# Layer-1 experts of a two-layer graph transformer: results added to rows of the output by accumulating scatters

## The chip, the cores and the metric

The kernel runs on one core of a Trainium2 chip. The metric is device time in microseconds (us), the median of several runs. The names used below: PE is TensorE (matrix products), DVE is VectorE, ACT is ScalarE, POOL is GpSimd and SP is SyncE, which here only issues loads. All engines read and write on-chip memory in tiles of 128 partitions (rows); matrix products land in PSUM banks. Transfers to and from DRAM are DMAs, issued by SP, ACT or POOL and carried out by 16 shared DMA engines. Every engine works through its own instructions in order. An instruction waits until the semaphores of what it needs have come.

## The reference

Two layers work on 384 nodes with 1024 features. Each layer adds a graph attention and a mixing block to x, and then a mixture of experts. All numbers are 32-bit floats. The change touches the experts of the second layer (layer 1), which the reference computes thus:

```python
aff = feats @ centroids.T
eid = jnp.argmax(aff, axis=1)
...
xhat = (feats - mu) * jax.lax.rsqrt(var + EPS)
out = jnp.zeros_like(feats)
for e in range(E):
    mask = (eid == e).astype(feats.dtype)[:, None]
    h = xhat * gamma[e] + beta[e]
    y = feats + jax.nn.relu(h @ w1[e] + b1[e]) @ w2[e] + b2[e]
    alpha = jax.nn.sigmoid(feats @ centroids[e])[:, None]
    out = out + mask * (alpha * y + (1.0 - alpha) * feats)
```

Here feats is the layer norm of x. Each node has exactly one of E = 8 experts, and the final output is x + out. For a node of expert e that comes to

x + feats + alpha * (relu(h @ w1[e] + b1[e]) @ w2[e] + b2[e]).

So there is a base, x + feats, which no expert touches, and a product scaled by alpha. The expert's bias b2[e] is scaled by alpha too.

## The kernel before, in words

**Blocks and places.** The 384 nodes lie in three blocks (nb) of 128 rows. The experts are worked sorted: every expert has CAP = 64 places, and a node's place (slot) is 64 * expert + its rank among the nodes of that expert. Two experts make a pair of 128 places, and four pairs follow each other. Places without a node keep a blank row index, so that what is written through them is dropped.

**Routing, at the end of `layer1`.** For a block, `project` multiplies by w_fc (L1117). `mix_norm` finishes x (L1128, L1129). `to_router` transposes x (`to_t`, L217 and L218), multiplies it by the centroids (L1151), and writes ft (feats) and xb (the normed feats). `to_places` finds the expert (one-hot oh, by `first_of`), the rank (`place`, a product with `later` or `ones_q`, L328), the slot and own (L1181, a one-hot over the 128 places of pair 0). It scatters xb by slot to the DRAM table xg. POOL then adds x + ft (L1184), and that base row is scattered by slot to the DRAM table bg. `to_first` multiplies xb by own (L1189), which gives pair 0's rows already transposed, in PSUM. In the code `to_router` of the last block comes first, then `to_first` of blocks 0 and 1, then `to_places` and `to_first` of the last. `scaled` (L974 and L975 on DVE, L981 on ACT) applies gamma and beta to pair 0's rows and writes xe0. Last, info, that is alpha and the node's row number, is scattered to ig.

**Experts, `experts1_sorted`.** POOL loads the four pairs' base rows back from bg (base) and loads ig (inf); ACT loads b2. For each pair the code runs:

- w1 of both experts is loaded by SP (`load_w`, 2 MB each).
- For pairs 1 to 3, xs is loaded by SP from xg and transposed (L1321), and `scaled` gives xeT. Pair 0 takes xe0.
- h = xeT * w1: 16 products (L1326). Each takes 64 places, and each appears in the profile as two passes, as 32-bit products do.
- ACT copies h to hs (L1329). It is transposed (L1335), and bias b1 and relu give hT (DVE L1343, ACT L1341).
- y = hT * w2 in two halves of 512 features, 8 products each (L1350). One more product per half adds b2 through `pick`, which names the expert of each place (L1352).
- o = y * alpha + base (L1354). One scatter by row number writes o to out (L292).

Each row of out is written once, by the pair that holds its node.

**The weight places.** `next_w` takes the 2 MB places for weights in turn from `ring`. Three stand in the ring from the start, and w_top, w_more (two) and w_last were added on the way, so that seven rotate here. A load can start when the last product that reads the place's former weights is done.

**Order.** A scheduler places the instructions of each engine. It may move work of one engine past other work, as the transposes L1321 of the next pair show, which stand ahead of y. `issue_after` sets an order by hand.

Of the kernel before, what the change touches and what calls it, by code (L numbers as in the profile page):

```python
# [10 lines left out]
F32 = mybir.dt.float32  # L11
I32 = mybir.dt.int32
AF = mybir.ActivationFunctionType
OP = mybir.AluOpType
# [30 lines left out]
def gps_two_layers(ctx: ExitStack, tc: tile.TileContext, d, out: bass.AP):  # L45
# [45 lines left out]
    bg = dram.tile([X * CAP, D], F32, name="bg")  # L91
    ig = dram.tile([X * CAP, 2], F32, name="ig")
    x1 = dram.tile([N, D], F32, name="x1")

# [151 lines left out]
    def first_of(onehot, vals, most):  # L246

        eq = small.tile([P, X], F32, tag="fo_e", name="fo_e")
        ve.scalar_tensor_tensor(eq, vals, most, ridx, op0=OP.is_equal, op1=OP.mult)
        c = small.tile([P, 1], F32, tag="fo_c", name="fo_c")  # L250
        ve.tensor_reduce(c, eq, AX.X, OP.max)
        ve.tensor_scalar(onehot, ridx, c, None, op0=OP.is_equal)

    def gate_to_t(pool, tag, gate):
        gT = small.tile([X, N], F32, tag="gT", name="gT", bufs=1)
# [29 lines left out]

    sent = {}

    def scatter(rows, ats, srcs, n):

        before = sent.setdefault(rows.tensor.name, [])  # L290
        for at, src in zip(ats, srcs):
            i = gp.indirect_dma_start(rows, bass.IndirectOffsetOnAxis(ap=at, axis=0), src, None,  # L292
                                      bounds_check=n - 1, oob_is_err=False)
            for j in before:
                tc.declare_no_dep(i.ins, j.ins, reason="no two nodes have one place")
            before.append(i)
        return i
# [15 lines left out]

    def blanks(q, blank):

        for t, n in ((xg0, X * CAP0), (xg, X * CAP), (bg, X * CAP)):
            for i in range(n // P):
                q.dma_start(t[i * P:(i + 1) * P, :], blank[:, :D])
        blank_i = const.tile([P, 2], I32, name="blank_i")
        gp.memset(blank_i, 1 << 20)  # L320
        for i in range(X * CAP // P):
            q.dma_start(ig[i * P:(i + 1) * P, :], blank_i.bitcast(F32))
# [91 lines left out]
    with ExitStack() as layer:  # L414
# [317 lines left out]
        def row(cols, name, dtype=F32):  # L732
            return kp.tile([P, *cols], dtype, name=name)

        keep = {"xe0": [row([KC // 2, P], f"xe0_{g}") for g in range(2)], "oh": row([NB, X], "oh4"), "own": row([NB, P], "own4"), "most": row([NB], "most4"),
                "slot": row([NB], "slot4", I32), "info": row([NB, 2], "info4"),
                "slots": row([NB, 2], "slots6", I32), "share": row([2, NB], "share6")}


# [243 lines left out]
    def layer1(keep=None):  # L983


        with tc.tile_pool(name="act2", bufs=1) as act, \
# [303 lines left out]

    def experts1_sorted(xe0):

        with tc.tile_pool(name="act4", bufs=1) as act, \
# [5 lines left out]
            b2 = act.tile([X, D], F32, name="b24")  # L1299
            ac.dma_start(b2, d["b2"])  # L1300
            pick = act.tile([X, X * CAP], F32, name="pick4")
            gp.tensor_copy(pick.rearrange("p (a b) -> p a b", b=CAP), ident[:X, :X][:, :, None].to_broadcast([X, X, CAP]))
            base = act.tile([P, X // 2, D], F32, name="base4")
            for pair in range(X // 2):
                gp.dma_start(base[:, pair, :], bg[pair * P:(pair + 1) * P, :])
                if pair == 0:
                    gp.dma_start(inf, ig.rearrange("(a p) b -> p a b", p=P))
            for pair in range(X // 2):
                es = (2 * pair, 2 * pair + 1)
                rows = slice(pair * P, (pair + 1) * P)  # L1310
                w1 = [load_w(d["xw1"][e]) for e in es]
                xeT = xe0
                if pair:
                    xs = work.tile([P, D], F32, tag="xs", name="xs4")
                    nc.sync.dma_start(xs, xg[rows, :])
                    xeT = [work.tile([P, KC // 2, P], F32, tag=f"xeT{g}", name="xeT4") for g in range(2)]
                    for g in range(2):
                        ps = pt.tile([P, HB], F32, tag="t", name="t4").rearrange("p (a b) -> p a b", b=P)
                        for j in range(4):
                            kc = g * 4 + j  # L1320
                            nc.tensor.transpose(ps[:, j, :], xs[:, kc * P:(kc + 1) * P], ident)  # L1321
                        scaled(xeT[g], ps, g, es)
                h = ph.tile([P, HB], F32, tag="h", name="h4")
                for kc in range(KC):
                    for r in range(2):
                        mm(h[r * CAP:(r + 1) * CAP, :], lhsT=xeT[kc // 4][:, kc % 4, r * CAP:(r + 1) * CAP], rhs=w1[r][:, kc, :],  # L1326
                           start=kc == 0, stop=kc == KC - 1)
                hs = work.tile([P, F1], F32, tag="hs", name="hs4")
                ac.copy(hs, h)  # L1329
                w2 = [load_w(d["xw2s"][e], (F1 // P, D)) for e in es]  # L1330
                hT = work.tile([P, F1 // P, P], F32, tag="hT", name="hT4")
                for g in range(2):
                    ps = pt.tile([P, HB], F32, tag="t", name="t4").rearrange("p (a b) -> p a b", b=P)
                    for j in range(2):
                        nc.tensor.transpose(ps[:, j, :], hs[:, (2 * g + j) * P:(2 * g + j + 1) * P], ident)  # L1335
                    for j in range(2):
                        for r, e in enumerate(es):
# [6 lines left out]
                y = [py.tile([P, HB], F32, tag="y", name="y4") for _ in range(2)]  # L1344
                o = work.tile([P, D], F32, tag="o", name="o4")
                for hf in range(2):
                    cs = slice(hf * HB, (hf + 1) * HB)
                    for j in range(F1 // P):
                        for r in range(2):
                            mm(y[hf][r * CAP:(r + 1) * CAP, :], lhsT=hT[:, j, r * CAP:(r + 1) * CAP],  # L1350
                               rhs=w2[r][:, j, cs], start=j == 0, stop=False)
                    mm(y[hf], lhsT=pick[:, pair * P:(pair + 1) * P],  # L1352
                       rhs=b2[:, cs], start=False, stop=True)
# [114 lines left out]
```

## Time and profile before

| what | us |
|---|---|
| median of 3 runs | 1074.85 |
| lowest and highest of them | 1074.51, 1077.58 |
| the profiled execution | 1074.58 |
| its span, first to last instruction | 1072.9 |
| PE busy | 1021.7 (95% of the span) |
| DVE, ACT, POOL busy | 346.0, 270.8, 317.8 |
| first expert product of layer 1 starts | 982.90 |
| first expert product of pairs 1, 2, 3 | 1004.99, 1026.79, 1047.17 |
| last product ends | 1065.38 |
| last scatter of out issued | 1066.45 |

The profile is of one execution. Its span leaves out 1.7 us of the time that was measured for that execution. Line numbers are those of the kernel before. "x32" counts instructions as the hardware ran them; a product of 32-bit floats counts as two. "Landing" is the time from the issue of a transfer to its completion. The granted clock is the share of full speed at which PE ran: 1.00 for most of the span, and 0.50 from 964 to 972 us.

### The profile page before, as it was taken

How to read it: one execution, taken by the hardware profiler on the slowest of the kernel's cores; microseconds unless marked ns; L12 is line 12 of the kernel's file. 1: busy time of each engine (PE TensorE's matmuls, PEld its weight loads, DVE VectorE, ACT ScalarE, POOL GpSimd, SP SyncE). 2: the span in 40 equal slices, each digit the busy share in tenths (PEclk: the TensorE clock that was granted, in tenths of full speed). 3: DMA queues.
4: the chain of work that ended last, by engine and by line, in shares of the span. 5: the costliest groups of instructions: out<-in, count | busy, mean ns of one | idle time of the engine just before them, and what ended most of it. 6: DMA issues, size and time to landing. Idle time of an engine off the chain costs nothing.

```text
span 1072.9 us, 9493 instructions
## 1 busy us (share of the span) xinstructions
PE 1021.7 (95%) x3453; PEld 554.1 (52%) x3453; DVE 346.0 (32%) x960; ACT 270.8 (25%) x499; POOL 317.8 (30%) x276
## 2 busy tenths in 40 slices
PE   6999999999999999999989999959999999988996
PEld 5555555544555555544466665424444466545332
DVE  4580000007676666701251110142205002463121
ACT  3111111100966666611131111221311111112111
POOL 2142365556685778500001000230002000024000
PEclk9999999999999999999999999979999999997999
DMA  9939623235326232541357888975540224244991
GB/s 346 402 126 391 199 79 134 102 103 102 75 1 158 33 47 1 158 162 44 128 206 261 312 303 309 361 260 205 195 141 17 78 83 153 79 170 148 392 411 59
DMA packets 69973, 186.01 MB, mean 173 GB/s; under 512 B 21416, under 2 KB 22280, under 8 KB 69664
## 3 DMA queue, kind: packets, MB, share of 16 engines
q1 hardware_dynamic: 41648, 149.68, 38.7%
q0 software_dynamic: 24688, 29.40, 11.1%
q10 hardware_dynamic: 3584, 6.25, 1.5%
q8 instruction: 29, 0.48, 0.2%
q14 instruction: 24, 0.20, 0.1%
HBM read 160.77 MB, written 25.06 MB: 173 GB/s over the span
## 4 chain that ended last, share of the span: by engine, by line
PE 92%; DVE 4%; DMA 1%; ACT 1%; issue 1%; POOL 0%; POOLq 0%; ACTq 0%; DVEq 0%
PE mm L136 23%; PE mm L148 12%; PE mm L666 11%; PE mm L714 8%; PE h L916 7%; PE mm L1012 4%; PE mm L1117 4%; PE y L943 4%; PE h L1326 3%; PE y L1350 3%; PE av L653 2%; PE sc L624 2%; PE tr L647 2%; PE x L1057 1%; PE mm L217 1%
## 5 line engine op out<-in xcount | busy, mean ns | idle before, releaser
L480 POOL DMA_INDIRECT countd<-seen,cells x96 | 153.9, 1603 | 64.4 <-DMA countd<-seen,cells 39.4
L136 PE MATMUL mm<-xnT,w 128*128 128x384 f32 x512 | 165.7, 486 | 0.0
L666 PE MATMUL mm<-xnT,w 128*128 128x384 f32 x384 | 132.4, 493 | 0.0
L136 PEld LDWEIGHTS mm<-xnT,w 128*128 128x128 f32 x512 | 97.1, 190 | 67.5
L480 POOL DMA_INDIRECT lastd<-typ,cells x96 | 95.7, 997 | 113.0 <-DMA lastd<-typ,cells 75.8
L666 PEld LDWEIGHTS mm<-xnT,w 128*128 128x128 f32 x384 | 70.5, 190 | 56.4 <-issue 13.4
L714 PE MATMUL mm<-w,t 128*128 128x512 f32 x192 | 84.3, 595 | 0.8 <-DVE x L402 0.8
L148 PE MATMUL mm<-w,xnT 128*128 128x512 f32 x192 | 82.8, 592 | 0.0
L136 PE MATMUL mm<-t,w 128*128 128x384 f32 x256 | 82.7, 486 | 0.0
L916 PE MATMUL h<-w,xeT 128*128 128x352 f32 x224 | 68.3, 462 | 0.7 <-DVE xeT L908 0.3
L136 PEld LDWEIGHTS mm<-t,w 128*128 128x128 f32 x256 | 48.6, 190 | 33.9
L148 PEld LDWEIGHTS mm<-w,xnT 128*128 128x128 f32 x192 | 36.3, 190 | 45.5 <-issue 45.5
L714 PEld LDWEIGHTS mm<-w,t 128*128 128x128 f32 x192 | 35.9, 190 | 44.1 <-issue 42.2
L586 DVE TENSOR_TENSOR kind<-last 128x1152 f32<-128x1152 f32 x1 | 1.4, 1358 | 167.7 <-DMA last<-lastd 167.7
L916 PEld LDWEIGHTS h<-w,xeT 128*128 128x128 f32 x224 | 41.9, 190 | 24.4 <-DVE xeT L908 2.4
L292 POOL DMA_INDIRECT xg<-xn,slot x3 | 4.0, 1324 | 144.0 <-DVE xn L1128 122.6
L1012 PE MATMUL mm<-w,xnT 128*128 128x512 f32 x96 | 43.7, 615 | 1.3 <-DVE xnT L218 1.3
L1117 PE MATMUL mm<-w,oT 128*128 128x512 f32 x96 | 42.6, 595 | 0.0
L943 PE MATMUL y<-w,hT 128*128 128x512 f32 (+1 forms) x96 | 41.6, 592 | 0.0
L148 PE MATMUL mm<-w,t 128*128 128x512 f32 x96 | 41.4, 592 | 0.0
L527 ACT ACTIVATE t<-mm,cols 128x384 f32<-128x384 f32 x24 | 13.9, 581 | 106.7 <-PE mm L136 106.7
L1067 POOL TENSOR_TENSOR x<-x,gb 128x1024 f32<-128x1024 f32 x3 | 7.3, 2423 | 99.2 <-DVE x L1066 99.2
(296 smaller groups left out, 1194.2 us busy)
## 6 DMA issues: line engine op xcount, KB each, us to landing
w<-in_w1s SPq DMA_DIRECT2D x16, 1408.0 KB, 7.1
w<-in_xw SPq DMA_DIRECT2D x8, 2048.0 KB, 12.3
w<-in_xw2s SPq DMA_DIRECT2D x8, 2048.0 KB, 13.7
w<-in_w2s SPq DMA_DIRECT2D x8, 1536.0 KB, 7.1
keys<-keyd POOLq DMA_DIRECT2D x4, 1536.0 KB, 14.3
xg<-blank SPq DMA_DIRECT2D x12, 512.0 KB, 11.0
w<-in_wk SPq DMA_DIRECT2D x2, 2048.0 KB, 15.8
w<-in_mwq SPq DMA_DIRECT2D x2, 2048.0 KB, 11.1
```

The costliest lines, as they stand in the source:

```text
L136: mm(ps[:, :N], lhsT=w[:, j, kc, :], rhs=rhs[:, kc, :], start=kc == 0, stop=kc == KC - 1)
L148: mm(ps, lhsT=lhs[:, kc, nb * P:(nb + 1) * P], rhs=w[:, kc, :], start=i == 0 and kc == 0, stop=i == len(pairs) - 1 and kc == KC - 1)
L480: gp.indirect_dma_start(cells[:, :], bass.IndirectOffsetOnAxis(ap=at[:, i, c:c + 1], axis=0), src[:, c:c + 1], None, bounds_check=N * N + ...
L624: mm(ps[:, r, :N], lhsT=q2T[rows, hp, nb * P:(nb + 1) * P], rhs=k2T[rows, hp, :], start=True, stop=True)
L666: mm(ps[:, :N], lhsT=w[:, j, kc, :], rhs=xnT[:, kc, :], start=kc == 0, stop=kc == KC - 1)
L714: mm(pss[hf], lhsT=src[:, kc, nb * P:(nb + 1) * P], rhs=w_out[("mwo", "wo")[part]][hf][:, kc, :], start=part == 0 and kc == 0, stop=part = ...
L916: mm(ag[i][:, :F0], lhsT=xeT[kc // 4][:, kc % 4, :], rhs=w1[kc // 4][:, kc % 4, i * F0:(i + 1) * F0], start=kc == 0, stop=kc == KC - 1)
L943: mm(y, lhsT=hT[:k, e, j, :], rhs=w2[:k, e % 2 * len(K2) + j, :], start=j == 0, stop=j == len(K2) - 1)
L1012: mm(ps, lhsT=xnT[:, kc, nb * P:(nb + 1) * P], rhs=ws[hf][:, kc, :], start=kc == 0, stop=kc == KC - 1)
L1117: mm(ps, lhsT=oT[:, kc, nb * P:(nb + 1) * P], rhs=ws[hf][:, kc, :], start=kc == 0, stop=kc == KC - 1)
L1326: mm(h[r * CAP:(r + 1) * CAP, :], lhsT=xeT[kc // 4][:, kc % 4, r * CAP:(r + 1) * CAP], rhs=w1[r][:, kc, :], start=kc == 0, stop=kc == KC - 1)
L1350: mm(y[hf][r * CAP:(r + 1) * CAP, :], lhsT=hT[:, j, r * CAP:(r + 1) * CAP], rhs=w2[r][:, j, cs], start=j == 0, stop=False)
```

## The change

The base rows are no longer sorted. The table bg is gone, with its blanks, its three scatters and its four loads. The base x + ft stays in on-chip memory in the order of the nodes: POOL makes it for blocks 0 and 1, DVE for the last block. Every node's own bias row is gathered from b2 by the expert's number (own_e), multiplied by alpha and added, and ACT stores the result to out. The experts then only *add* to out: y * alpha goes out by scatters with compute_op add, two per pair, one for each half of 512 features (half holds 2 * row + half). They wait for the three base stores. The product with `pick` is gone.

`to_first` of block 0 now stands before the last `to_router`, and that of block 1 right behind it. The rows of all pairs are loaded early, by POOL and no longer by SP. The next pair's rows are transposed inside the y of pair 0, and between h and hs of pairs 1 and 2. The copy hs is divided between DVE and ACT. The ring gets one more place, w_end.

```diff
 def first_of(onehot, vals, most):
...
+        return c
...
-    def scatter(rows, ats, srcs, n):
+    def scatter(rows, ats, srcs, n, op=OP.bypass):
...
-                                      bounds_check=n - 1, oob_is_err=False)
+                                      bounds_check=n - 1, oob_is_err=False, compute_op=op)
...
-        for t, n in ((xg0, X * CAP0), (xg, X * CAP), (bg, X * CAP)):
+        for t, n in ((xg0, X * CAP0), (xg, X * CAP)):
...
-                first_of(oh[:, nb, :], near, top)
+                c = first_of(oh[:, nb, :], near, top)
...
-                with tc.issue_after(scatter(xg[:, :], [slot[:, nb:nb + 1]], [xb], X * CAP).ins):
-                    gp.tensor_tensor(x[:, nb, :], x[:, nb, :], fb, OP.add)
-                    last[:] = [scatter(bg[:, :], [slot[:, nb:nb + 1]], [x[:, nb, :]], X * CAP)]
+                ve.tensor_scalar(keep["own_e"][:, nb:nb + 1], c, -1.0, float(X), op0=OP.mult, op1=OP.add)
+                last[:] = [scatter(xg[:, :], [slot[:, nb:nb + 1]], [xb], X * CAP)]
+                if nb < NB - 1:
+                    with tc.issue_after(last[0].ins):
+                        gp.tensor_tensor(x[:, nb, :], x[:, nb, :], fb, OP.add)
...
+            to_first(0)
             to_router(NB - 1)
-            for nb in range(NB - 1):
-                to_first(nb)
+            to_first(1)
             to_places(NB - 1)
             to_first(NB - 1)
...
+            ve.tensor_tensor(x[:, NB - 1, :], x[:, NB - 1, :], ft[:, NB - 1, :D], OP.add)
...
+            ring.append(w_end)
...
+            def load_rows(pair):
+                xs = work.tile([P, D], F32, tag="xs", name="xs4", bufs=3)
+                gp.dma_start(xs, xg[pair * P:(pair + 1) * P, :])
+                return xs
...
+            def hidden_of(pair, xeT):
...
-                ac.copy(hs, h)
+                ve.tensor_copy(hs[:, :F1 // 2], h[:, :F1 // 2])
+                ac.copy(hs[:, F1 // 2:], h[:, F1 // 2:])
...
+            def give(pair, hT, between=None):
...
-                    mm(y[hf], lhsT=pick[:, pair * P:(pair + 1) * P],
-                       rhs=b2[:, cs], start=False, stop=True)
-                    ve.scalar_tensor_tensor(o[:, cs], y[hf], inf[:, pair, 0:1], base[:, pair, cs],
-                                            op0=OP.mult, op1=OP.add)
-                scatter(out[:, :], [inf[:, pair, 1:2].bitcast(I32)], [o], N)
+                    o = work.tile([P, HB], F32, tag="o", name="o4", bufs=4)
+                    ve.tensor_scalar(o, y, inf[:, pair, 0:1], None, op0=OP.mult)
+                    scatter(out.rearrange("n (h f) -> (n h) f", h=2), [half[:, hf, pair:pair + 1]], [o], 2 * N, OP.add)
+                    if hf == 0 and between is not None:
+                        got = rows_of(between)
...
+            xss = [None] + [load_rows(pair) for pair in range(1, X // 2)]
+            gp.dma_start(inf, ig.rearrange("(a p) b -> p a b", p=P))
+            for nb in range(NB):
+                gather(b2[:, nb, :], d["b2"], keep["own_e"][:, nb:nb + 1], X)
+            hs = hidden_of(0, xe0)
+            for hf in range(2):
+                ve.tensor_scalar(half[:, hf, :], inf[:, :, 1].bitcast(I32), 2.0, float(hf), op0=OP.mult, op1=OP.add)
+            for nb in range(NB):
+                ve.scalar_tensor_tensor(x[:, nb, :], b2[:, nb, :], keep["info"][:, nb, 0:1], x[:, nb, :],
+                                        op0=OP.mult, op1=OP.add)
+                ac.dma_start(out[nb * P:(nb + 1) * P, :], x[:, nb, :])
+            xeT = give(0, by_feature(0, hs), 1)
+            for pair in range(1, X // 2):
+                hs = hidden_of(pair, xeT)
+                if pair + 1 < X // 2:
+                    xeT = rows_of(pair + 1)
+                give(pair, by_feature(pair, hs))
```

In the built program the new instructions stand thus on their engines: on DVE the two `half` steps ahead of pair 0's hs, the first addition of a bias row between the second and third hT piece of pair 0, the other two around the first scaling step of pair 1's rows; on ACT the base stores behind pair 0's hT, among the scaling steps of pair 1's rows; on POOL, after the last scatters to xg and ig, the loads xs, inf, the three gathers and the scatters of out.

More of the change, by code (lines that the diff above doesn't have):

```diff
@@ L90, in gps_two_layers @@
     xg = dram.tile([X * CAP, D], F32, name="xg")
-    bg = dram.tile([X * CAP, D], F32, name="bg")
     ig = dram.tile([X * CAP, 2], F32, name="ig")
@@ L735, in gps_two_layers @@
         keep = {"xe0": [row([KC // 2, P], f"xe0_{g}") for g in range(2)], "oh": row([NB, X], "oh4"), "own": row([NB, P], "own4"), "most": row([NB], "most4"),
-                "slot": row([NB], "slot4", I32), "info": row([NB, 2], "info4"),
+                "slot": row([NB], "slot4", I32), "own_e": row([NB], "own_e4", I32), "info": row([NB, 2], "info4"),
                 "slots": row([NB, 2], "slots6", I32), "share": row([2, NB], "share6")}
@@ L1291, in experts1_sorted @@
     def experts1_sorted(xe0):
-        with tc.tile_pool(name="act4", bufs=1) as act, \
+        with tc.tile_pool(name="w_end", bufs=1) as w_end, \
+                tc.tile_pool(name="act4", bufs=1) as act, \
                 tc.tile_pool(name="work5", bufs=2) as work, \
@@ L1297, in experts1_sorted @@
                 tc.tile_pool(name="ps_y4", bufs=2, space=PSUM) as py:
+            ring.append(w_end)
             inf = act.tile([P, X // 2, 2], F32, name="inf4")
[L1299 to L1322, printed above, removed]
+            half = act.tile([P, 2, X // 2], I32, name="half4")
@@ new lines, in experts1_sorted, with rows_of @@
+            b2 = act.tile([P, NB, D], F32, name="b24")
+            def load_rows(pair):
+                xs = work.tile([P, D], F32, tag="xs", name="xs4", bufs=3)
+                gp.dma_start(xs, xg[pair * P:(pair + 1) * P, :])
+                return xs
+            def rows_of(pair):
+                xeT = [work.tile([P, KC // 2, P], F32, tag=f"xeT{g}", name="xeT4") for g in range(2)]
+                for g in range(2):
+                    ps = pt.tile([P, HB], F32, tag="t", name="t4").rearrange("p (a b) -> p a b", b=P)
+                    for j in range(4):
+                        kc = g * 4 + j
+                        nc.tensor.transpose(ps[:, j, :], xss[pair][:, kc * P:(kc + 1) * P], ident)
+                    scaled(xeT[g], ps, g, (2 * pair, 2 * pair + 1))
+                return xeT
@@ L1323, in experts1_sorted @@
+            def hidden_of(pair, xeT):
+                w1 = [load_w(d["xw1"][e]) for e in (2 * pair, 2 * pair + 1)]
                 h = ph.tile([P, HB], F32, tag="h", name="h4")
@@ L1328, in experts1_sorted, with by_feature @@
                 hs = work.tile([P, F1], F32, tag="hs", name="hs4")
-                ac.copy(hs, h)
-                w2 = [load_w(d["xw2s"][e], (F1 // P, D)) for e in es]
+                ve.tensor_copy(hs[:, :F1 // 2], h[:, :F1 // 2])
+                ac.copy(hs[:, F1 // 2:], h[:, F1 // 2:])
+                return hs
+            def by_feature(pair, hs):
                 hT = work.tile([P, F1 // P, P], F32, tag="hT", name="hT4")
@@ L1336, in experts1_sorted @@
                     for j in range(2):
-                        for r, e in enumerate(es):
+                        for r, e in enumerate((2 * pair, 2 * pair + 1)):
                             f, cs = 2 * g + j, slice(r * CAP, (r + 1) * CAP)
@@ L1343, in experts1_sorted @@
                                 ve.tensor_scalar(hT[:, f, cs], ps[:, j, cs], bias, 0.0, op0=OP.add, op1=OP.max)
-                y = [py.tile([P, HB], F32, tag="y", name="y4") for _ in range(2)]
-                o = work.tile([P, D], F32, tag="o", name="o4")
+                return hT
+            def give(pair, hT, between=None):
+                w2 = [load_w(d["xw2s"][e], (F1 // P, D)) for e in (2 * pair, 2 * pair + 1)]
                 for hf in range(2):
                     cs = slice(hf * HB, (hf + 1) * HB)
+                    y = py.tile([P, HB], F32, tag="y", name="y4")
@@ L1348, in experts1_sorted @@
                     for j in range(F1 // P):
                         for r in range(2):
-                            mm(y[hf][r * CAP:(r + 1) * CAP, :], lhsT=hT[:, j, r * CAP:(r + 1) * CAP],
-                               rhs=w2[r][:, j, cs], start=j == 0, stop=False)
-                    mm(y[hf], lhsT=pick[:, pair * P:(pair + 1) * P],
-                       rhs=b2[:, cs], start=False, stop=True)
-                    ve.scalar_tensor_tensor(o[:, cs], y[hf], inf[:, pair, 0:1], base[:, pair, cs],
-                                            op0=OP.mult, op1=OP.add)
@@ L1356, in experts1_sorted @@
-                scatter(out[:, :], [inf[:, pair, 1:2].bitcast(I32)], [o], N)
+                            mm(y[r * CAP:(r + 1) * CAP, :], lhsT=hT[:, j, r * CAP:(r + 1) * CAP],
+                               rhs=w2[r][:, j, cs], start=j == 0, stop=j == F1 // P - 1)
+                    o = work.tile([P, HB], F32, tag="o", name="o4", bufs=4)
+                    ve.tensor_scalar(o, y, inf[:, pair, 0:1], None, op0=OP.mult)
+                    scatter(out.rearrange("n (h f) -> (n h) f", h=2), [half[:, hf, pair:pair + 1]], [o], 2 * N, OP.add)
@@ new lines, in give @@
+                    if hf == 0 and between is not None:
+                        got = rows_of(between)
+                return got if between is not None else None
+            xss = [None] + [load_rows(pair) for pair in range(1, X // 2)]
[5 more added lines that the diff above has]
+                ve.tensor_scalar(half[:, hf, :], inf[:, :, 1].bitcast(I32), 2.0, float(hf), op0=OP.mult, op1=OP.add)
```

## The prediction

> **What bounds the kernel now.** I read the page's chain first, then the chain in order of time from 960 us, the waits of PE, and last the stretches with the DMA share.
>
> ```profile
> PE 92%; DVE 4%; DMA 1%; ACT 1%; issue 1%; POOL 0%; POOLq 0%; ACTq 0%; DVEq 0%
> ```
>
> PE holds 92% of the chain, so time is saved where PE loses work or a wait, and nowhere else. The change lies in the last 110 us. There the chain in order of time (start, length, what) runs:
>
> ```profile
> 970.91 4.94 PE first L1189 x30
> ...
> 979.91 2.75 DVE xe L975
> ...
> 1013.65 0.59 ACT hs L1329
> ...
> 1039.32 1.05 PE y L1352 x2
> 1040.37 3.58 PE y L1350 x16
> 1043.95 1.06 PE y L1352 x2
> ...
> 1046.43 0.70 DVE xeT L975
> 1047.17 7.14 PE h L1326 x32
> ```
>
> The reader is to see four kinds of loss: 30 `first` passes ahead of the last ranks; an add of 2.75 us that takes 0.69 elsewhere; a bias product of 1.05 us per half; and short pieces of DVE and ACT between products. The waits of PE from 850 us (total, times, longest) give these pieces a size:
>
> ```profile
> PE h L1326 <- DVE xeT L975: 3.9, 3, 1.4
> PE mm L217 <- DVE x L1129: 3.8, 1, 3.8
> PE h L1326 <- DVE xe L975: 2.9, 1, 2.9
> PE t L1335 <- ACT hs L1329: 2.1, 3, 0.7
> ```
>
> No wait there is on a load. Yet the DMA engines are full while the experts run (columns: stretch, length, five engines' busy time, clock, DMA share, GB/s):
>
> ```profile
> 1005.00:1047.00 42.00, 38.00 (x160) 14.63 (x160) 7.18 (x16) 7.54 (x25) 1.93 (x2) 0.96 1.02 408
> ```
>
> The weights are thus a second bound close behind PE: the last 2 MB load was issued at 1033.9, landed 17.7 us later at 1051.6, and its first product ran at about 1055.9.
>
> **The routing of the last block (before the first expert product).** The new order puts the `first` products of blocks 0 and 1 into the 3.8 us in which PE waits for x, instead of behind the router product. DVE is ready with x at 965.05 as now. `first` of 15 matmuls costs about 4 us at full clock (16 passes took 2.05), from 960.6, with own of block 1 at 962.95: PE reaches the transposes at 964.9, the second half at 965.6, the copy xT at 966.3. The router product (16 passes, 1.7 at full clock as in block 0) ends at 968.1, against 970.9. The seven small DVE steps to the one-hot end at 969.3, and `rank` runs at once: now it waits behind the `first` passes until 975.85. Ten more DVE steps, with one of 0.54, give the last own at 971.8 (now 977.93) and the eight `first` of block 2 end at 973.9. Then xe: multiply 0.69; the block's add x + ft, which moves from POOL to DVE and stands between (two of the 0.69 rows, 1.4, on the path); the add at 0.69 and not 2.75, since POOL's add (2.37 us, 979.72 to 982.1, exactly beside the slow one) is gone. That ends at 975.6; ACT's half (8 x 0.31) at 976.4, so the first product starts at **976.5 instead of 982.9: 6.4 gained**. Bounds 4 and 7.5: half clock, as now from 964 to 974 (0.50), costs up to 2.
>
> **Pair 0: where the change adds waits.** POOL's queue now holds, in order: the last xg scatter (972.7, landing 3.3 as its row), three ig scatters (1.28 apart, last issued 976.5), three loads xs (0.55 each, moved here from SP), inf, three gathers of b2, and then the scatters of out. The w_end load (SP) waits for the same xg scatter and for PE, DVE and POOL; it starts at about 976.2. inf waits for the last ig to land (rows 4.3 to 6.5; I take 6, beside the weight load): issued at 982.5, behind 1.57 MB of xs. Together with w_end's 2.1 MB that is 3.67 MB, 9 us at 0.41 MB/us, so inf lands at about **987** (bounds 985 and 990).
>
> On DVE `half` waits for inf, and the hs copy, which pair 0's transposes need, stands behind `half`. The product h0 ends between 983.6 and 985.3 (7.1 at full clock, 8.8 as now), so this new wait costs PE about 2.5. After the first two hT pieces DVE waits for gather 0 and only then does the other two; the scaling of pair 1's rows stands behind gathers 1 and 2 on DVE, and behind the two or three base stores on ACT. Gathers are 0.52 MB each, issued 983.6 to 986.2, beside two weight loads from 984.5. The nearest row is base, of the same size in the same company: landings 4.1, 8.1, about 10 and 12.3. At half of 410 GB/s I get 990, 993.5 and 996.5. Then the chain is: gather 2, the add of x 1.4 (two of the 0.75 rows), o 0.7, xeT 0.7: 999.3. PE's own road (y resumes at 992, 14 matmuls of 0.45) ends at 998.2. So h1 starts at **1000, against 1004.99** (bounds 994.5, no stall; 1005, gathers landing like the last base).
>
> Rule against row: the skill's DMA: Bandwidth & Descriptors, section SWDGE vs HWDGE vs iDMA, sends plain loads to SP or ACT; its Specifications put the first byte at about 1 us from POOL and 0.6 from SP, 0.4 dearer for what is behind xs. The rows show 4.6 to 5.4 for SP's xs and 4.1 for POOL's first base, so nothing by the row, 0.4 by the rule. I take the row: the cost of the move is the place in the queue, counted above.
>
> **Pairs 1 to 3.** Per pair now 20.4 at full clock. The bias products go: 2 x 1.05 = 2.1 a pair (8.4 in all, 2.1 of it in pair 0). The transposes of the next rows stand where PE waits for hs and hT, and xeT is ready before y ends: 1.36 goes. hs in two halves of 256 (about 0.37 each, DVE then ACT) hides behind the transposes. New: DVE's scaling steps stand between hs and hT (0.69 twice), leaving some 0.5. I get h 7.1, 1.6 to 2.0 of transposes and hT, y 16 x 0.45 = 7.2: 16.35, 16.2, and 15.45 for the last, which has no next rows. From h1 to the end of y: **48.0 instead of 60.4** (1004.99 to 1065.38, in which the half clock took 1.5). PE alone would end at 1048, with y3 beginning at 1040.8.
>
> **The weights.** From 976.2 on must land: w_end 2.1, xs, gathers and base stores 1.57 each, eight weights 16.8, and four accumulating scatters of 0.26 each. The trace shows an accumulating load of 0.59 MB (ed_w, L1018), 12.4 us against 7.2 for the plain one:
>
> ```profile
> 716.50:729.00 12.50, 1.00 1.05 347
> 729.00:735.00 6.00, 1.00 1.03 419
> ```
>
> The engines are full, but 72 GB/s less arrive for 12.5 us, 0.9 MB: an accumulated byte costs some 2.5 plain ones. So 23.6 + 1.05 x 2.5 = 26.2 MB. Before, 23.1 MB took from 991.7 to 1051.6, 0.385 MB/us: 68 us, last landing 1044, 3 us after PE wants it. With the bare 0.41 it is 1040, no wait. The eighth place (seven rotate now) brings loads forward by one turn but makes no bandwidth. I take 2 us of wait: y ends at 1050.
>
> **Tail.** From y to the span's end now 7.5. The last scatter carries half the bytes, the other half left 3 us earlier. Its price: landing 3.3 for 0.52 MB. The skill's fit (same page, Anatomy of one DMA — SWDGE (gpsimd) path: 2.0 + bytes/436e3 per us) makes 2.6 of 0.26 MB, blind to the add; the ed_w rows make up to 3.3 - 0.6 + 5.2 x 0.26/0.59 = 5.0. POOL's small accumulating scatters (1.55 against 0.98 issue, landing about 0.8 later) are nearer: 3.9. Tail 8.2.
>
> **At nothing.** Four bg blanks leave SP's queue at about 90 us: PE runs the L136 products there without a wait on a load, so 0; bare, their four issues of 0.32 would give 1.3. own_e adds three DVE steps of 0.15, in the figures above. The first scatter of out waits for the three base stores, until about 1008; behind it on POOL stand only the other scatters, and o has four buffers, the fifth wanted at 1029. Without that cover DVE would stall, and PE behind it through the two y banks.
>
> **Sum.** 1050 + 8.2 = 1058.2 span; outside it 1074.58 - 1072.9 = 1.7: **1060 us**, 14.6 below the profiled 1074.58. The median 1074.85 is 0.3 higher, inside the rounding.
>
> **Rivals.**
> - *Cover complete* (0.14): inf and gathers land early as base's first did, PE keeps full clock, accumulation costs no more than a plain byte. h1 at 994.5, y at 1043, then 1053. For it: DMA is idle from 972 to 980 now. Against: the weights must land 4 us before the estimate.
> - *POOL's queue late* (0.22): ig and inf behind 3.67 MB, gathers at 12 to 15 us; h1 at 1005, half clock 1.5, y at 1055: 1066. For it: xs from SP took 15.6 us at 1024.
> - *Slower: accumulation chokes the loads* (0.06). Place: pair 3's w2, behind the scatters of pairs 0 and 1. The last landing is 976.2 + (23.6 + 1.05 k)/0.385, k the price of an accumulated byte. y3 must slip from 1040.8 to 1057.5 to lose all, so from k = 7.3 on; at k = 10, with the tail's scatter 3 us slower, 1085. The trace has 2.5.
> - *No net change* (0.02): late gathers and k near 7 just cancel, 1074.6.
> - The *forecast* keeps 0.56.
>
> Range: 1053 holds the cover case, 1067 the late queue; about 0.1 lies on each side. Faster by over 0.3% (3.2 us, about what can be told from no change) 0.92, within 0.02, slower 0.06.
>
> **What would show it.** In the changed profile: no `pick` product; first h at 976 to 978 with clock 1.00 over 964 to 974; the xe add at 0.7; PE's wait for hs in pair 0 ended by inf, then y or h1 by a gather of b2; periods of 16 to 17 us from pair 1; weights as PE's releaser before y3 for 0 to 3 us; the last out scatter landing near 4 us. Wrong if h0 starts after 980, if h1 starts after 1006, or if PE waits over 6 us on loads of w.

## The result, and the profile after

| | before | after |
|---|---|---|
| median of 6 runs | 1077.28 us | 1067.63 us |
| lowest and highest | 1074.51, 1079.11 | 1065.68, 1070.25 |
| profiled execution (its span) | 1074.58 (1072.9) | 1067.88 (1066.2) |

The ratio is 0.9915, with a 95% interval of 0.9895 to 0.9936: 9 to 10 us are gained, where the forecast had 14.6. The time lies 0.6 us above the end of the range.

The two profiled executions cannot be laid over each other as they are. At the start of the changed part the new one is already 3.4 us late, and that comes from work which the change doesn't touch: after two older gaps of PE (near 560 and 700 us) the half clock lasted some 4 us longer, to about 572 and 719 instead of 568 and 714. Four of the experiments below, with the same code up to there, start early, as the execution before did; two made in the kernel before start late. So every stretch below is counted from the first of the `first` products (963.84 us here), which the prediction had at 960.6.

PE's own timeline, of the kernel after (start, length, what; in brackets the idle time before it and what ended it):

```profile
975.35 3.47 PE L1190 MATMUL first<-own,xn 128*128 128x128 f32 x16 [1.18 <-DVE slot L1181]
981.38 8.78 PE L1326 MATMUL h<-w,xe 128*64 128x512 f32 x32 [2.56 <-ACT xe L980]
...
994.00 0.84 PE L1338 MATMUL t<-ident,hs 128*128 128x128 f32 x4 [3.84 <-issue]
...
1005.53 7.09 PE L1326 MATMUL h<-w,xeT 128*64 128x512 f32 x32 [0.83 <-DVE xeT L974]
...
1046.68 1.93 PE L1357 MATMUL y<-w,hT 128*64 128x512 f32 x4
1050.46 7.05 PE L1357 MATMUL y<-w,hT 128*64 128x512 f32 x28 [1.85 <-SPq L1392]
```

The bias products are gone, and the next pair's rows no longer stop PE behind pair 0. Three new things are there. The last 16 `first` passes take 3.47 us where they took 2.05, at half clock (0.50 from 972 to 978 us). PE stands 3.84 us ahead of pair 0's transposes. And the last y waits for SP's queue, that is for the last weights.

Who is behind the 3.84 us ("issue" names no one), DVE's timeline of the kernel after tells:

```profile
993.33 0.24 DVE L1372 TENSOR_SCALAR half<-inf 128x4 int32<-128x4 int32 x2 [13.45 <-DMA b<-in_b,own_e]
993.48 0.42 DVE L1329 COPY hs<-h 128x256 f32<-128x256 f32 x1
...
995.94 1.28 DVE L1374 SCALAR_TENSOR_TENSOR x<-b,info,x 128x1024 f32<-128x1024 f32 x1 [1.02 <-DMA b<-in_b,own_e]
...
1002.93 1.28 DVE L1374 SCALAR_TENSOR_TENSOR x<-b,info,x 128x1024 f32<-128x1024 f32 x1 [1.58 <-DMA b<-in_b,own_e]
```

The copy hs starts the moment `half` is through, 0.5 us ahead of PE's transposes, though h had been ready since 990.2. The bracket names a gather of b2, but `half` reads inf and not b2, and in the runs 3 and 4 below the bracket of `half` does name inf; so the wait is taken to be on inf. Then each of the three additions of a bias row (two are shown) waits for its gather, as forecast. The DMA engines in the stretch that was shown of before, and then at the end of the loads (stretch, length, busy time of five engines, clock, DMA share, GB/s):

```profile
1005.00:1047.00 42.00, 40.79 (x189) 20.14 (x190) 10.26 (x25) 9.46 (x35) 9.36 (x6) 1.00 1.02 377
```

```profile
1044.00:1046.00 2.00, 1.41 (x6) 0.34 (x3) 0.42 (x1) 0.23 (x1) 0.00 (x0) 1.00 0.91 263
1046.00:1048.00 2.00, 1.96 (x7) 0.67 (x6) 0.86 (x4) 1.07 (x5) 0.00 (x0) 1.00 0.63 219
1048.00:1050.00 2.00, 0.61 (x2) 0.00 (x0) 0.00 (x0) 0.00 (x0) 0.00 (x0) 1.00 0.27 111
```

The engines are as full as before (1.02) and carry less (377 GB/s against 408). PE is now busy 40.79 of 42 us, where it was 38.00. In the last 6 us the mean share falls while the last load is still under way; it landed at about 1050.4, when the last y could go on.

### The profile page after: what moved, and what is told of

Read it like the earlier page. It is cut to its first block, busy times and chain, and to the rows that moved or that the text cites. A ratio compares the mean times of both kernels' runs of the same rounds, so it can differ in the third digit from the quotient of the medians.

```text
span 1066.2 us, 9480 instructions
## 1 busy us (share of the span) xinstructions
PE 1017.0 (95%) x3437; PEld 554.8 (52%) x3437; DVE 350.4 (33%) x973; ACT 269.7 (25%) x499; POOL 321.9 (30%) x277
```

## The experiments

Two theories stood against each other. **Theory A**: pair 0's new waits, on inf and the gathers, decide the end. **Theory B**: the landing of the last weights does, so that a stall of PE in pair 0 only stands in the place of a wait on weights later. The table divides each run at the same points: from the first `first` product to h of pair 0, from there to h of pair 1, from there to the end of the last y, and from there to the span's end. The ratios are to the kernel before, timed beside it. The four stretches are from one profiled execution of each run, the medians and ratios from five or more executions.

| run | median us | ratio, 95% interval | routing | pair 0 | pairs 1-3 | tail |
|---|---|---|---|---|---|---|
| forecast | 1060 | | 15.9 | 23.5 | 50.0 | 8.2 |
| after | 1067.63 | 0.9915, 0.9895-0.9936 | 17.5 | 24.2 | 52.0 | 8.7 |
| late adds | 1066.49 | 0.9909, 0.9877-0.9941 | 17.4 | 18.1 | 56.7 | 8.7 |
| plain scatters | 1061.76 | 0.9866, 0.9832-0.9899 | 17.5 | 23.1 | 48.9 | 7.8 |
| no w_end | 1069.63 | 0.9932, 0.9913-0.9951 | 17.4 | 19.7 | 58.7 | 8.8 |
| rows by SP | 1074.15 | 0.9968, 0.9950-0.9985 | 18.0 | 33.7 | 48.4 | 8.7 |
| deferred scatters | 1065.86 | 0.9895, 0.9875-0.9915 | 17.5 | 25.0 | 48.5 | 10.1 |
| late adds + deferred | 1060.51 | 0.9840, 0.9824-0.9857 | 17.4 | 19.8 | 49.2 | 9.0 |
| the same, PE's gaps filled | 1062.20 | 0.9864, 0.9840-0.9887 | 21.5 | 16.7 | 48.8 | 9.3 |
| the same, no w_end | 1060.20 | 0.9866, 0.9842-0.9891 | 17.4 | 18.2 | 52.9 | 10.0 |
| the same, let go early | 1068.85 | 0.9920, 0.9891-0.9950 | 17.5 | 18.5 | 59.3 | 8.8 |

**1. Late adds: the stall taken out of pair 0.**

```diff
-            for hf in range(2):
-                ve.tensor_scalar(half[:, hf, :], inf[:, :, 1].bitcast(I32), 2.0, float(hf), op0=OP.mult, op1=OP.add)
-            for nb in range(NB):
...
-                ac.dma_start(out[nb * P:(nb + 1) * P, :], x[:, nb, :])
             xeT = give(0, by_feature(0, hs), 1)
+            with tc.issue_after(made[-1][2].ins):
+                for hf in range(2):
+                    ve.tensor_scalar(half[:, hf, :], inf[:, :, 1].bitcast(I32), 2.0, float(hf), op0=OP.mult, op1=OP.add)
+                for nb in range(NB):
...
+                    ac.dma_start(out[nb * P:(nb + 1) * P, :], x[:, nb, :])
+            spill()
```

`made` collects the o steps, and `spill` issues the scatters of those collected.

> The changed kernel, but the two half steps, the three additions of a bias row, the base stores and pair 0's scatters stand behind pair 0's o. So hs, hT and the scaling of pair 1's rows no longer stand behind inf and the gathers on DVE and ACT. Theory A (pair 0's new waits decide the end): PE's 3.84 us behind hs shrinks below 1, first h to first h of pair 1 falls from 24.2 us to about 19.5, and the time is 4 to 5 us below the changed kernel: ratio to the kernel before near 0.987. Theory B (the landing of the last weights decides the end): first h to first h of pair 1 falls just as much, but PE's wait on the weight queue grows from 1.85 us to 5 to 7 us in the last pair, and the time is within 1 us of the changed kernel: ratio 0.9915.

PE's timeline of this run, pair 0 and pair 3:

```profile
986.98 0.84 PE L1338 MATMUL t<-ident,hs 128*128 128x128 f32 x4 [0.71 <-DVE hs L1329]
...
995.96 7.04 PE L1326 MATMUL h<-w,xeT 128*64 128x512 f32 x32
...
1034.31 9.21 PE L1326 MATMUL h<-w,xeT 128*64 128x512 f32 x30 [5.54 <-SPq L1402]
```

Pair 0 shrank from 24.2 to 18.1 us, 6.0 less, and pairs 1 to 3 grew by 4.8. The wait of 1.85 us in pair 3's y is gone, and one of 5.54 us stands in front of pair 3's h. It costs more than itself: the clock was at 0.50 from 1032 to 1038 us, and this h took 9.21 us, where 30 passes behind a wait of 0.61 us (run 11) took 7.08. The median is 1.1 us lower, and the two intervals overlap: no gain is shown. That is Theory B, in the wait and in its size.

**2. Plain scatters: the price of the addition.**

```diff
-                    scatter(out.rearrange("n (h f) -> (n h) f", h=2), [half[:, hf, pair:pair + 1]], [o], 2 * N, OP.add)
+                    scatter(out.rearrange("n (h f) -> (n h) f", h=2), [half[:, hf, pair:pair + 1]], [o], 2 * N)
```

> The changed kernel with the scatters of out writing instead of adding (out then lacks x, feats and the bias; the same bytes leave on-chip memory). Price of an accumulation by itself. Theory B: at 1.8 plain bytes for an accumulated one the loads get 0.84 MB, at 0.385 MB/us 2.2 us, back: PE's wait of 1.85 us on the weights in the last pair goes, the tail (last y to the span's end, 8.7) shrinks by about 0.5: 2 to 2.5 us below the changed kernel, ratio near 0.9893. If an accumulated byte costs 2.5, as forecast, the gain in the loads is 4 us, but PE can take no more than the same 1.85. If accumulation costs no more than a write, the time does not move (ratio 0.9915). Theory A expects the tail's 0.5 alone.

The gain is 5.3 us by the ratios, over twice what was expected: 3.1 in pairs 1 to 3, 0.9 in the tail, 1.1 in pair 0. No wait on weights is left. How dear the addition is, the DMA queues of the two kernels show for the same stretch, 1000 to 1066 us (queue, kind: packets, MB, share of 16 engines' time). First the kernel after, then this run (its span ends at 1059.1):

```profile
q1 hardware_dynamic: 3829, 15.16, 57.0%
q0 software_dynamic: 1233, 1.84, 15.7%
```

```profile
q0 software_dynamic: 640, 1.57, 6.1%
```

q1 carries the weights, q0 what POOL issued. A weight byte costs 57.0 / 15.16 = 3.8% per MB, a plain scattered one 6.1 / 1.57 = 3.9%. After has 0.27 MB of the last gather in that stretch; without it the adding scatters cost (15.7 - 1.05) / 1.57 = 9.3% per MB. So **an added byte costs 2.4 to 2.5 plain ones**, the 2.5 that the prediction took from ed_w. The 1.8 of the expectation was too low.

**3. Without w_end**, seven places as before.

```diff
-        with tc.tile_pool(name="w_end", bufs=1) as w_end, \
-                tc.tile_pool(name="act4", bufs=1) as act, \
+        with tc.tile_pool(name="act4", bufs=1) as act, \
...
-            ring.append(w_end)
```

> The changed kernel without w_end (seven places rotate, as before). Theory B: 2.1 MB lose the start in the idle time of the DMA engines at 976 to 984 and are sent later, up to 5 us of the loads; the last landing slips and PE's wait on weights in the last pair grows from 1.85 us to 4 to 7: the time is 2 to 5 us above the changed kernel, ratio 0.993 to 0.996. Theory A (and the forecast, which gave the place nothing of its own): inf and ig land 1 to 3 us earlier because less moves beside them, h1 starts that much earlier, time 0 to 2 us below the changed kernel.

Both expectations came true in part. POOL's timeline of this run:

```profile
976.83 0.97 POOL L291 DMA_INDIRECT ig<-info,slot  x1 [0.30 <-issue]
...
980.78 0.77 POOL L1365 DMA_DIRECT2D inf<-ig  x1 [1.32 <-DMA ig<-info,slot]
```

and of the kernel after:

```profile
980.43 0.97 POOL L291 DMA_INDIRECT ig<-info,slot  x1 [0.30 <-issue]
...
988.19 0.77 POOL L1367 DMA_DIRECT2D inf<-ig  x1 [5.12 <-DMA ig<-info,slot]
```

From the issue of the last ig scatter to the issue of inf it is 3.95 us here and 7.76 there. The load into w_end starts in exactly this gap, at 979.67, so it makes ig late, and with it inf, `half` and hs: pair 0's stall is the place's doing (0.67 us of it left here). But without the place PE waits 3.12, 2.76 and 2.27 us for weights in pairs 2 and 3, and by the ratios the whole is 1.8 us slower. The two intervals overlap, so that the place gives more than it takes is likely, but not shown.

**4. Rows by SP**, as the kernel before had it.

```diff
-                gp.dma_start(xs, xg[pair * P:(pair + 1) * P, :])
+                nc.sync.dma_start(xs, xg[pair * P:(pair + 1) * P, :])
```

> The changed kernel with the three loads xs issued by SP, as in the kernel before, so that POOL has only inf and the gathers behind the last ig scatter. Theory A: inf (5.1 us from issue to landing in the changed kernel, behind 1.57 MB of xs in POOL's queue) lands 2 to 3 us earlier, PE's wait of 3.84 us for hs falls to 1 to 2 us, the time is 2 to 3 us below the changed kernel, ratio near 0.989. Theory B: pair 0 gets shorter by as much, and the time stays (ratio 0.9915), the wait on weights before the last y growing by 2.

This missed both, since the run tests something else: with other costs in the queue the scheduler put one gather ahead of inf, and all three additions ahead of hs. DVE's timeline of this run:

```profile
991.18 1.29 DVE L1374 SCALAR_TENSOR_TENSOR x<-b,info,x 128x1024 f32<-128x1024 f32 x1 [11.32 <-DMA b<-in_b,own_e]
...
1000.62 1.28 DVE L1374 SCALAR_TENSOR_TENSOR x<-b,info,x 128x1024 f32<-128x1024 f32 x1 [2.79 <-DMA b<-in_b,own_e]
1001.82 0.42 DVE L1329 COPY hs<-h 128x256 f32<-128x256 f32 x1
```

PE stood 12.0 us in front of its transposes instead of 3.8, and this run loses 5.7 us against after. It still tells two things. The place of the loads xs in POOL's queue is at most a small part of what made inf late: inf was issued 7.0 us after the last ig scatter (7.8 in the kernel after), and `half` started 12.3 us after pair 0's h (12.0). And the run is a third point on one line: a stall of 0.7, 3.8 and 12.0 us in pair 0 goes with a wait on weights of 5.5, 1.85 and none later. Pair 0 and pairs 1 to 3 together take 74.9, 76.1 and 82.1 us: of the first 3.1 us of stall 1.3 show, of the next 8.2 it is 6.0.

**5 and 6. Parts of the change made in the kernel before**: the order of the first products alone, and the bias product left out alone.

```diff
+            to_first(0)
             to_router(NB - 1)
-            for nb in range(NB - 1):
-                to_first(nb)
+            to_first(1)
             to_places(NB - 1)
```

> The kernel before with nothing changed but the order of the first products (block 0 ahead of the last router product, block 1 right behind it). The routing step of the prediction by itself: 6.4 us of it, without the two parts that belong to the base rows (the add of 2.75 us stays: 2.06 less gained; no x+ft on DVE: 1.4 more), so 5.7 us by the prediction. The changed kernel showed about 5 (half clock in the last first products). The first expert product then starts at 977 to 978 instead of 982.9, and since all loads follow the places that PE frees, the end moves with it: 4.5 to 5.7 us below the kernel before, ratio 0.9947 to 0.9958. A rival: the loads, full from 990 us on, do not move, and the gain is eaten by a wait on weights: 0 to 2 us.

Measured: 1071.06 against 1076.91 us, ratio 0.9941 (0.9924 to 0.9957): 5.9 us less by the medians, 6.4 by the ratio, with the 5.7 expected inside the interval. In the profiled executions the routing gives 4.9 of it (from the last `rank` ahead of the `first` products to pair 0's h 17.8 us instead of 22.7). Another 1.5 is the half clock that the kernel before had in pair 1's h (8.58 us, here 7.09). No wait on weights came. The last first products, in PE's timeline of this run, are slow here too:

```profile
975.42 3.57 PE L1189 MATMUL first<-own,xn 128*128 128x128 f32 x16 [1.18 <-DVE slot L1182]
```

```diff
-                               rhs=w2[r][:, j, cs], start=j == 0, stop=False)
-                    mm(y[hf], lhsT=pick[:, pair * P:(pair + 1) * P],
-                       rhs=b2[:, cs], start=False, stop=True)
+                               rhs=w2[r][:, j, cs], start=j == 0, stop=j == F1 // P - 1)
```

> The kernel before without the product that adds b2 (the output lacks b2). PE has 8.4 us less to do, and DMA nothing less and nothing more. Theory A (PE is the bound): 8 us below the kernel before, ratio 0.9925, no wait on weights. Theory B (the loads are a bound close behind PE): the last 2 MB, landed at 1051.6 and used from 1055.9, leave 4.3 us; 4 to 5 us below, ratio 0.9955, and PE shows a wait of 3 to 4 us that is ended by a load of w in pair 3.

Measured: 1070.79 us, ratio 0.9938 (0.9917 to 0.9958), 6.7 us less by the ratio and 6.1 by the medians, between the two. The waits of PE in this run have one new row, and its last first products are slow, with the old order:

```profile
PE t L1321 <- SPq L1364: 1.6, 1, 1.6
```

```profile
982.20 3.67 PE L1189 MATMUL first<-own,xn 128*128 128x128 f32 x16 [0.89 <-DVE slot L1182]
```

8.4 us of products left and 1.6 came back on the weights: 6.8. The second bound was near, but the loads gave way further than the 4.3 us read from the last landing. They also started earlier: the last one was issued 45.1 us after the start of pair 0's h, before 51.0.

**7 and 8. Scatters held back, alone and with the late adds.** The results of pairs 0 to 2 stay on the chip, and one adding scatter for each goes out once hs of pair 3 is copied.

```diff
+                        if hf == 0:
+                            o = b2[:, pair, :]
+                            held_back.append((pair, o))
...
+                    with tc.issue_after(copies[-1].ins):
+                        ve.tensor_copy(node_of, inf[:, :, 1].bitcast(I32))
+                    for back, o in held_back:
+                        scatter(out[:, :], [node_of[:, back:back + 1]], [o], N, OP.add)
```

> The changed kernel with the adding scatters of pairs 0 to 2 held until pair 3's hs is copied (one scatter of whole rows for each pair, 128 x 1024), so that the last weights need not share the DMA engines with them. Pair 0's waits stay as they are (3.8 us behind hs). Theory B: some 1.2 MB of accumulated rows leave the time of the loads, at 1.8 plain bytes each 2.1 MB or 5 us, so the wait of 1.85 us on the last weights goes and the first passes of the last y run at their full rate: 2 to 4 us below the changed kernel, ratio 0.988 to 0.9897. Theory A: 0 to 1 us below (no wait of pair 0 goes).

> Both: the additions of the bias and the base stores behind pair 0's o, as in the run late_adds, and the scatters of pairs 0 to 2 held until pair 3's hs. Theory B: late_adds gave 6.0 us in pair 0 and lost 5.5 to a wait on weights; without the scatters beside them the loads have 23.6 MB from 976 us on, at 0.40 MB/us until about 1035, where PE wants the last w2 at 1037: the wait falls to 0 to 2 us, and the time is 5 to 7 us below the changed kernel, ratio 0.985 to 0.987. If the scatters' accumulation is not what fills the DMA engines, the wait stays above 4 us and the ratio at 0.990.

Held alone: the wait on weights is gone and pairs 1 to 3 take 48.5 us instead of 52.0, but the tail grew by 1.4 and pair 0 by 0.8: about 2 us by the ratios, at the low end of what was expected, and with overlapping intervals. Both together reach **1060.51 us, ratio 0.9840 (0.9824 to 0.9857)**, 7 to 8 us below after, a little more than expected, and faster than both kernels. No wait on weights is left in it; the late adds alone had given 1 us. The DMA engines of this run, where the loads end and the held scatters begin:

```profile
1034.00:1036.00 2.00, 2.00 (x13) 0.80 (x9) 0.00 (x0) 0.00 (x0) 0.00 (x0) 1.00 1.03 412
...
1040.00:1042.00 2.00, 2.00 (x12) 1.25 (x10) 0.00 (x0) 0.00 (x0) 1.70 (x2) 1.00 1.04 137
1042.00:1044.00 2.00, 2.00 (x12) 1.33 (x10) 0.75 (x1) 0.00 (x0) 1.25 (x1) 1.00 1.02 148
```

The share is full in the first row and in the last two, with 412 GB/s of weights and 137 to 148 GB/s of added rows: an addition seen by itself, at 2.8 to 3.0 plain bytes. (These are whole rows of 4 KB, those of the kernel after half rows.)

**9. The gaps of PE filled.** Eight products into an unused tile, to hold the clock up.

```diff
-            to_first(NB - 1)
+            fill(3, ranked[0])
+            fill(5, to_first(NB - 1))
```

> The kernel of the run late_deferred with eight products into an unused PSUM tile: three behind the last rank (PE idles 1.4 us there) and five behind the last first products (PE idles 2.6 us there). Clock theory: the half clock from 970 to 983 us, which every run with the new order of the first products shows, comes from these gaps. With them filled, the last 16 first passes take 2.05 us instead of 3.8, h of pair 0 7.1 instead of 8.4 to 10.1, and the first product starts about 1.5 us earlier: 3 to 4.5 us below late_deferred, ratio 0.980 to 0.9815. Rival: the clock falls for another reason (the load of the two dense places before, the share of small products), then the eight products only push work back: 0 to 1.5 us above late_deferred, ratio 0.984 to 0.9855. A third: pair 0 gets faster, but the loads cannot follow (last landing 1037.3, wanted at 1038.5), so a wait on weights of 2 to 3 us takes most of it: 0 to 1.5 us below.

The clock theory was wrong: no gain is shown, and the ratio is 2.6 us worse, a little more than the rival expected, with overlapping intervals. PE's timeline of this run:

```profile
975.39 5.33 PE L1200 MATMUL idle<-x,ident 128*128 128x512 f32 x6
980.56 1.95 PE L1192 MATMUL first<-own,xn 128*128 128x128 f32 x16
...
987.23 7.09 PE L1337 MATMUL h<-w,xe 128*64 128x512 f32 x32 [0.30 <-issue]
```

The later products ran at full clock: `first` 1.95 us, h 7.09. But the clock had fallen all the same, to 0.50 from about 974 to 980 us. It fell before the first filler began (975.39), and the first three fillers took 5.33 us instead of the 1.4 planned. Routing grew by 4.1 us, pair 0 shrank by 3.0. So the two gaps, which lie behind the fall, are not what lowers the clock; what does stays open.

**10 and 11. The better version without w_end (the edit of run 3), and with the scatters let go early**, of which this is the edit:

```diff
-                    with tc.issue_after(copies[-1].ins):
+                    with tc.issue_after(made[-1].ins):
```

> The kernel of the run late_deferred with seven places instead of eight (no w_end). In the changed kernel the place cost PE 3 us behind hs, since its load moved beside ig, and brought about 6 us of loads forward, 1.9 us net. Here nothing in pair 0 waits for ig or inf, so the place can only help: without it 2.1 MB, 5 us at 0.40 MB/us, come later, against 1 us of slack: 3 to 5 us above late_deferred, ratio 0.987 to 0.9885, with 3 to 6 us of waits on loads of w in pairs 2 and 3. If PE alone is the bound there, the time stays at 0.984.

> The kernel of the run late_deferred with the held scatters of pairs 0 to 2 let go one step earlier, behind pair 2's last o (7 us before pair 3's hs). Their rows then move beside the last weights: at 145 GB/s for accumulated rows against 410 for loads, 1.2 MB of them take 8 us of the DMA engines. If the accumulation is what delayed the loads in the changed kernel, the last landing slips from 1037.3 to 1040 to 1045 and PE waits 2 to 6 us for the last w2, while the tail behind the last y shrinks from 9.0 to about 8: 1 to 4 us above late_deferred, ratio 0.985 to 0.988. If not, the tail alone counts: 0.5 to 1 us below, ratio 0.983.

Without w_end one wait of 2.57 us on weights came back, and pairs 1 to 3 took 3.7 us more. Pair 0 took 1.6 less, but all of that lies in its h, which had half clock for less time (8.47 us against 10.09). The median is the same as with it, the ratio 2.8 us worse, and the intervals overlap: unclear. Letting the scatters go some 7 us earlier cost 8.6 us by the ratios, far more than expected. The waits of PE in that run:

```profile
PE y L1360 <- SPq L1407: 6.8, 1, 6.8
```

and its DMA engines:

```profile
1038.00:1040.00 2.00, 2.00 (x11) 0.58 (x8) 0.00 (x0) 0.00 (x0) 1.36 (x1) 1.00 1.10 346
...
1042.00:1044.00 2.00, 1.95 (x5) 0.47 (x4) 0.61 (x4) 0.93 (x4) 0.00 (x0) 1.00 1.09 270
```

The same bytes, moved beside the last weights instead of behind them, make PE wait 6.8 us, and the 28 passes of y behind that wait, in part at half clock, took 8.57. Where the additions are placed decides here, not how many there are.

## Why the prediction was wrong

The mechanisms were those forecast, in their order. The sum missed by 4.8 us, in four terms that all fell on the same side: routing 1.6, pair 0 0.7, pairs 1 to 3 2.0, tail 0.5. The profiled span ended at 1066.2 instead of 1058.2, and the other 3.2 of these 8.0 us lie ahead of the change: the `first` products began at 963.84 where the prediction had 960.6. It took the time up to there from the one profiled execution before, without a margin. The four terms alone would have ended at about 1065 us and the late start alone at about 1063, both inside the range; together they are above it. Of the prediction's own signs of being wrong one came true as written, pair 0's h after 980 (981.38); counted from the same start it is 978.1.

**Routing, "976.5 instead of 982.9: 6.4 gained"**: half right. The waits left as forecast, the xe add took 0.69, the base add of the last block 1.22. What failed is the choice between the bounds: "half clock, as now from 964 to 974 (0.50), costs up to 2" was taken at zero, for which the prediction gives no reason. The clock fell to 0.50 all the same, only later, from 972 to 978, and this stretch gained 4.9 us instead of 6.4. Every run with the new order shows the fall, and the last 16 passes take 3.5 to 3.8 us in all of them but the filled one. The run without the bias product shows it with the old order (3.67 us), so the fall does not need the new order. The Trainium skill (TensorE: Matmul & The Clock Gate, The HAM clock gate) has the full clock come after about 3.4 us of sustained work. In the filled run PE was busy without a break from 974 to 980, and the clock stayed at 0.50 for some 6.8 us, twice as long as the page has it.

**Pair 0, "h1 starts at 1000"**: 0.7 off, with the parts shifted. "inf waits for the last ig to land ... I take 6": it took 7.8, since w_end's load fell into the same gap; the load was foreseen and its effect sized too small. PE's wait behind it, put at "about 2.5", was 3.84. Counted from h0, inf landed 1.3 later than forecast and the last gather 1.4 later; the steps behind that gather took 2.6 instead of 3.5.

**Pairs 1 to 3, "48.0 instead of 60.4", "I take 2 us of wait: y ends at 1050"**: this is the step that failed most. PE alone takes 48.4 to 49.2 us, as the runs without waits on weights show; 0.4 to 1.2 more than the 48.0. The last y, begun and broken off, took 10.8 us from its first pass to its last, against 7.7 in the run with plain scatters: 3.1 for a wait put at 2.

Behind that wait stands the sum of the loads. The price k of 2.5 was right. The last landing came out at 1044, "3 us after PE wants it"; counted from the same start it was 1047. The sum has "four accumulating scatters of 0.26 each", those of pairs 0 and 1. But by the prediction's own times pair 2's y ends more than 10 us ahead of that landing, so its two scatters move beside the loads too. In the kernel after they were issued 14 and 11 us ahead of it:

```profile
1036.08 1.54 POOL L291 DMA_INDIRECT out<-o,half  x1 [11.35 <-DVE o L1360]
1039.40 1.54 POOL L291 DMA_INDIRECT out<-o,half  x1 [1.79 <-DVE o L1360]
```

With six instead of four, at the prediction's 0.26 MB, 2.5 and 0.385 MB/us, the landing comes to 1047.7. By the DMA queues the six carried only about 1.2 MB, since places without a node are dropped, which makes 1045.3. So the two scatters are 1 us of the 3 by the bytes that moved, and all of them by the prediction's own count. Another 0.9 us is the rate: where the prediction has 23.1 MB from 991.7 to 1051.6, the trace has 22.76. The last 1 us was not separated. The fall of the mean share ahead of the landing (0.91, 0.63, 0.27) is not the cause. In the kernel before it was as long, and the 0.385, taken over that stretch, has it in it:

```profile
1046.00:1048.00 2.00, 0.86 (x5) 0.34 (x6) 1.08 (x2) 1.87 (x7) 0.96 (x1) 1.00 0.86 344
1048.00:1050.00 2.00, 2.00 (x12) 0.72 (x10) 0.00 (x0) 0.61 (x3) 0.00 (x0) 1.00 0.52 211
1050.00:1052.00 2.00, 2.00 (x12) 0.63 (x10) 0.00 (x0) 0.00 (x0) 0.00 (x0) 1.00 0.08 31
```

**Tail, 8.2**: 8.7. Plain scatters make 7.8, so the addition costs 0.9 there; the prediction gave the whole tail 0.7 over before's 7.5.

**Weights as a second bound**: right, and it is the larger lesson. That the wait on weights and pair 0's stall replace each other is in the prediction's sum, where the landing does not move with pair 0. The runs give it its size: taking the stall out gave 1 us, holding the scatters back gave 2 (neither clear of the noise), both gave 7 to 8.

Of the rivals, the late POOL queue comes nearest in the total (1066), in part by luck: it has pair 1's h at 1005, where it was at 1002.3 counted from the same start, and the late start is not in it. Its cause is half right: w_end's load did hold up ig and inf, the place of xs in the queue hardly (run 4). Choking of the loads (break-even at k = 7.3) did not come to pass in this placing. The run with the scatters let go early shows that its mechanism is real at k = 2.5 already, when they meet the last loads: 6.8 us.

## What to carry to other kernels

Where an engine and the DMA engines are both nearly full, as here, a gain in one is paid out only up to the slack of the other: test each repair together with the other one before dropping it. Count an accumulating scatter at some 2.5 times its bytes (2.4 to 3.0 here), count every one that is issued ahead of the landing in question, and place it where no load is waited for. Take the start of the changed stretch from more than one execution. In an in-order engine a small step that waits for a transfer (`half`, a bias add) holds everything behind it; put it behind the copies that the bound engine needs.

## What the hardware showed beside that

- Added rows by themselves moved at 137 to 162 GB/s with the DMA engines full (1040 to 1046 us of late adds + deferred), weights just before at 401 to 412 (1022 to 1036).
- POOL spends 1.54 to 1.63 us on the issue of an adding scatter, 0.97 to 1.02 on the same one without the addition.
- With the new order the clock fell to 0.50 in every run, 8 to 10 us after the first of the `first` products and for 6 to 14 us, whatever stood in PE's gaps. In the two profiles with the old order it fell too, from 964 to 972 us (before) and from about 969 to 979 (bias left out). Why it falls there was not found.
- A wait of PE on weights can cost more than its length: behind waits of 2.57, 5.54 and 6.80 us (runs 10, 1 and 11) the clock was at 0.50 for 3 to 7 us. Behind those of 1.85 (after), 2.27, 2.76 and 3.12 us (run 3) it was not.
- The DMA engines don't end together: the mean share falls for 2 us (plain scatters) to 6 us (after, and before too) ahead of the last landing.
